# When a gate is made, where a bias row is multiplied, and where the last block's statistics and sums stand, in a conditioned two-layer block

## The chip, the cores and the metric

The kernel runs on one core of one Trainium2 chip. The core has TensorE (PE in the profile; PEld is its weight load), VectorE (DVE), ScalarE (ACT), GpSimd (POOL) and SyncE (SP), and 16 DMA engines. Each engine works through its own list of instructions in the order in which the program emits them. The metric is device time in microseconds, the median over runs.

## The reference

The input x has two batch entries of 2048 rows of 512 numbers, float32; each entry has a condition vector of 512.

```python
emb = jnp.dot(jax.nn.silu(t), ada_w) + ada_b
shift_msa, scale_msa, gate_msa, shift_mlp, scale_mlp, gate_mlp = jnp.split(emb, 6, axis=-1)
norm = _ln(x) * (1.0 + scale_msa[:, None]) + shift_msa[:, None]
h = jax.nn.gelu(jnp.dot(norm, ssm_w1) + ssm_b1, approximate=False)
x = x + gate_msa[:, None] * (jnp.dot(h, ssm_w2) + ssm_b2)
norm2 = _ln(x) * (1.0 + scale_mlp[:, None]) + shift_mlp[:, None]
hf = jax.nn.gelu(jnp.dot(norm2, ff_w1) + ff_b1, approximate=True)
x = x + gate_mlp[:, None] * (jnp.dot(hf, ff_w2) + ff_b2)
```

ssm_w1 and ssm_w2 are 512 x 512, ff_w1 is 512 x 1024, ff_w2 is 1024 x 512. Shift, scale and gate differ between the two batch entries and are the same for all rows of one. The kernel numbers the six parts of emb 0 to 5; the gates are parts 2 and 5.

## The kernel before

**Blocks and stages.** The 4096 rows are cut into eight blocks of 512; blocks 0 to 3 are batch entry 0, blocks 4 to 7 entry 1. A block i goes through four matmul stages. hA_i is norm times w1 with the first gelu. oA_i is that times w2, added to x. hC_i is the second norm times fw1 with the second gelu, in two groups of the hidden dimension. oC_i is that times fw2, added to x. The order on PE is hA_0, oA_0, hA_1, and then, for i from 0, hC_i (both groups), oA_{i+1}, oC_i, hA_{i+2}. At i = 6 there is no later hA, and oA_7 stands between the two groups of hC_6.

**Seven products.** Every stage multiplies 2 x 2 blocks with seven products P1 to P7 instead of eight (`group`, L275). Sums of quarters of the operands are formed beforehand by four additions on DVE or GpSimd (`sums_of_first`, `sums_of_second`; lines 215 to 218 and 225 to 228). The products accumulate in three PSUM banks called y, x and v: P1, P6, P7 and P4 all add into y, P2 is alone in x, P5 and P3 add into v. Partial results are read out between products, so a product that adds into a bank waits for the eviction that reads the bank's earlier state. In a hidden stage (`hidden`) DVE evicts s1 after P1 (L455) and completes it after P2 (L457), evicts u2 after P6 (L461) and completes it after P3 (L469), evicts s5 after P5 (L464) and completes it after P7 (L466); after P4 ScalarE reads the bank itself (L473). In a residual stage (`residual`) DVE adds each product's bank to x (L501). The products of most stages run in the order P1, P2, P6, P5, P7, P3, P4; the first two hidden stages and oA_0 in FIRST: P1, P2, P5, P6, P7, P3, P4.

**What sets the order.** The order is written out by hand. `hook(hooks, places, ops)` hangs other work behind a product: the operations are emitted after that product's eviction, so each engine meets them there in its own list. With more operations than places, the rest go to the last place.

**Norms.** `Norm.stats` is four statistics on DVE (L327, L328). `scales` is eight small operations on GpSimd (L336 to L354). `normal` is four instructions on ScalarE (L367). For the first blocks PE then transposes (`transpose`, L396). For later ones DVE transposes small squares (`turn`, L378), 16 DMAs on the sync queue move them (`move`, L387), and ScalarE applies scale and shift in place (`moved`, L410). `summed` forms the operand sums.

**Gates.** The gate of a part is a 512-long row for each batch entry. It is folded into the weights: w2 (and fw2) are multiplied column by column, and so is the bias row. `ada_rows` (L154) makes four partial sums for both entries with four matmuls, and adds the bias. `gates` (L198) picks and adds up one entry's rows with one matmul over 512 columns, which leaves the gate on all 128 partitions in a PSUM tile of the pool ps_t. For entry 1 it is copied into SBUF by ScalarE (L205). Both entries' gates are made at the beginning: part 2 in hA_0, part 5 in the first group of hC_0. `weight_of_second` (L253) multiplies the weights by the gate (L258) and forms the operand sums on GpSimd. When the blocks pass to entry 1, the weights are loaded afresh and folded with its gate: w2 (`refold2`) is loaded in oC_2 and folded on GpSimd during hA_4; fw2 (`refold5`) is loaded after oC_3 and folded on DVE from hC_4 on. `gate_bias` (L517) loads the bias row (`load_row`, L122) and multiplies it by the gate on GpSimd (L520); `biases` (L510) adds the product to x, four operations on GpSimd (L513). For entry 0 the row's product stands in `ssm_gate` (L643) and `gb5_0`.

Of the kernel before, what the change touches and what calls it, by code (L numbers as in the profile page):

```python
# [43 lines left out]
def kernel(  # L44
# [102 lines left out]
    load_x(1)  # L147
    b2_bc = work.tile([P, D], F32, tag="gb", name="gb2_0", bufs=2)
    load_row(b2_bc, b2)
    load_ada(3)  # L150
    load_ada(4)
    fw1_sb = load_w("fw1", fw1)

    def ada_rows(g, bias):  # L154

        pa = ps_g.tile([P, D], F32, tag="x", name=f"pada_{g}")
        for k in range(KD):
            nc.tensor.matmul(
                pa[k * G : (k + 1) * G, :],
                silu[:, k, :],  # L160
                ada[g][:, k, :],
                start=True,
                stop=True,
                tile_position=(0, k * G),
            )
        t = work.tile([P, D], F32, tag="tmp", name=f"adarows_{g}", bufs=4)
        nc.vector.tensor_tensor(t, pa, bias, ALU.add)
        return t
# [27 lines left out]
    gate = {}  # L196

    def gates(g, b, sums_g):  # L198

        pg = ps_t.tile([P, D], F32, tag="t", name=f"pgate_{g}_{b}")  # L200
        nc.tensor.matmul(pg, pick_bc[:, b, :], sums_g, start=True, stop=True)
        gate[g, b] = pg
        if b:
            gate[g, b] = work.tile([P, D], F32, tag="gate", name=f"gate_{g}_{b}", bufs=2)
            nc.scalar.activation(gate[g, b], pg, AF.Identity)  # L205
# [311 lines left out]
    def gate_bias(gt, row, name):  # L517
        t = work.tile([P, D], F32, tag="gb", name=name, bufs=2)
        load_row(t, row)
        nc.gpsimd.tensor_tensor(t, gt, t, ALU.mult)  # L520
        return t
# [118 lines left out]
    def ssm_gate():  # L640
        gates(2, 0, found["rows"])
        found["w2"] = weight_of_second(w2_sb, w2_s, gate[2, 0], (nc.vector,))
        nc.vector.tensor_tensor(b2_bc, gate[2, 0], b2_bc, ALU.mult)  # L643

    def fold2(lo, hi):
        return [lambda k=k: found["w2"][1][k]() for k in range(lo, hi)]
# [3 lines left out]
    hook(hooks, ("P2",), [lambda: found.update(rows=ada_rows(2, brows[:, 0, :]))] + n1_sums[3:])  # L650
    st = n1[1].stats()
    hook(hooks, ("P5",), [ssm_gate] + biases(0, b2_bc) + fold2(0, 2))
    hook(hooks, ("P6",), [lambda: gates(2, 1, found["rows"])] + fold2(2, 7))
    hook(hooks, ("P7",), st[:2])
    hook(hooks, ("P3",), st[2:])
    hA[0] = First(0, n1[0].ops, hooks, FIRST)
# [5 lines left out]

    hook(hooks, ("P2",), hA_sums[2:] + [lambda: modulation(3, 0)])
    hook(hooks, ("P2",), [lambda c=c: n1[1].normal(c, on_pe=True) for c in range(C)])
# [14 lines left out]
    hook(hooks, ("P6",), [lambda: found.update(rows=ada_rows(5, brows[:, 1, :]))])  # L679
# [3 lines left out]
    def ff_gate():  # L683
        for b in reversed(range(B)):
            gates(5, b, found["rows"])
        found["fw2"] = weight_of_second(fw2_sb, fw2_s, gate[5, 0], (nc.vector,))
# [21 lines left out]
    for i in range(NBLK):  # L708
# [46 lines left out]
        early = nxt and not nx2  # L755
        hooks = {}
# [37 lines left out]
        if nxt:  # L794
            run(n2[i + 1].summed(nc.vector if early else nc.gpsimd))

        refold5 = (i + 1) % PER_B == 0 and nxt
        if refold5:
            load_w("fw2", fw2, fw2_sb)
            gb[5] = gate_bias(gate[5, (i + 1) // PER_B], fb2, "gb5_1")  # L800
            fw2_ops, fold = weight_of_second(
                fw2_sb, fw2_s, gate[5, (i + 1) // PER_B], (nc.vector,)
            )
# [56 lines left out]
```

## Time and profile before

| | us |
|---|---|
| median of 3 runs | 616.57 (616.48 to 619.3) |
| the profiled execution | 616.38 |
| its span | 614.6 |
| hA_0 and oA_0 on PE | 14.5 to 47.2 |
| first product of hC_0 | from 63.8 |
| oC_2, then hA_4 | from 246.8, then from 271.0 |
| oC_3 ends, hA_5 follows | 343.5 |
| oA_7 ends, the second group of hC_6 follows | 524.8 |
| oC_6 ends, hC_7 follows | 562.0 |

A line of a group or of the timeline gives start and length (or busy time), engine, source line and operation, what it writes and reads with shapes, and in brackets the idle time before it and what ended it. The name of a tile carries its stage: py_hA is bank y of a hidden stage A. A group of a stage with four matmuls shows as x8, since one float32 matmul is two instructions here.

### The profile page before, as it was taken

The numbers are of one execution on the slowest core, as the hardware profiler recorded it, in microseconds if no ns is written. First come the engines' busy times: TensorE is split into PE (matmuls) and PEld (weight loads), VectorE is DVE, ScalarE is ACT, GpSimd is POOL, SyncE is SP. The second block draws the span as 40 slices with busy tenths as digits, with TensorE's granted clock in tenths as the row PEclk, the third lists the DMA queues.
The fourth block names the chain that finished last, engine by engine and source line by source line (L and its number), as shares of the span: only waits on it lengthen the run. The fifth ranks groups of instructions, "written<-read, shape, count | busy, mean of one in ns | idle before, by whom it ended". The sixth has DMA issues, their size and how long they took to land.

```text
span 614.6 us, 7849 instructions
## 1 busy us (share of the span) xinstructions
PE 604.0 (98%) x2899; PEld 522.5 (85%) x2899; DVE 296.3 (48%) x506; ACT 174.0 (28%) x261; POOL 354.2 (58%) x366
## 2 busy tenths in 40 slices
PE   7899999999999999999999999999999999999997
PEld 4687888888888888888888888888888888888886
DVE  5867685335553355523563367633556233714322
ACT  3234341143330531322232333115233131320110
POOL 2796489755634853549948368966555393160330
PEclk9999999999999999999999999999999999999999
DMA  8961002240113302351021820224010400021001
GB/s 326 414 254 69 1 6 64 52 154 1 28 42 78 128 2 64 91 146 61 1 68 36 251 75 18 51 63 143 1 46 24 138 1 1 6 63 68 1 2 69
DMA packets 22075, 47.74 MB, mean 78 GB/s; under 512 B 4068, under 2 KB 4624, under 8 KB 21140
## 3 DMA queue, kind: packets, MB, share of 16 engines
q1 hardware_dynamic: 21952, 47.20, 24.3%
q8 instruction: 23, 0.38, 0.3%
q14 instruction: 16, 0.13, 0.1%
q10 hardware_dynamic: 84, 0.03, 0.0%
HBM read 25.20 MB, written 8.39 MB: 55 GB/s over the span
## 4 chain that ended last, share of the span: by engine, by line
PE 92%; DMA 3%; DVE 2%; ACT 1%; SPq 1%; POOL 0%; issue 0%; ACTq 0%; DVEq 0%; POOLq 0%
PE py_oC L290 18%; PE py_hC L290 18%; PE pv_hC L290 9%; PE py_oA L290 9%; PE pv_oC L290 9%; PE py_hA L290 8%; PE pv_oA L290 5%; PE px_oC L290 4%; PE px_hC L290 4%; PE pv_hA L290 4%; PE px_oA L290 2%; DMA gb<-in_L_cond_ssm_b_dram 2%; PE px_hA L290 2%; DMA rows<-in_L_cond_ff_b_dram 1%; DVE st L327 0%; PE pt L396 0%
## 5 line engine op out<-in xcount | busy, mean ns | idle before, releaser
L410 ACT ACTIVATE nT<-nT,mod,mod 128x512 f32<-128x512 f32 x52 | 38.1, 802 | 165.1 <-DMA nT<-blocks 127.0
L513 POOL TENSOR_TENSOR x<-x,gb 128x512 f32<-128x512 f32 x64 | 79.4, 1272 | 4.0 <-issue 3.9
L215 POOL TENSOR_TENSOR hSC<-hClo 128x512 f32<-128x512 f32 x16 | 20.8, 1301 | 75.5 <-ACT hClo L450 75.5
L290 PE MATMUL py_hC<-nS,fw_s 128*128 128x256 f32 x256 | 60.7, 380 | 1.0 <-DVE s1hC L455 1.0
L367 ACT ACTIVATE nT<-x,nmr,rstd 128x512 f32<-128x512 f32 x52 | 38.7, 803 | 69.7 <-POOL nmr L354 69.7
L290 PE MATMUL py_oC<-fw_s,hSC 128*128 128x256 f32 x256 | 57.9, 379 | 0.0
L290 PEld LDWEIGHTS py_hC<-nS,fw_s 128*128 128x128 f32 x256 | 48.5, 190 | 8.3 <-DVE s1hC L455 1.8
L290 PEld LDWEIGHTS py_oC<-fw_s,hSC 128*128 128x128 f32 x256 | 48.6, 190 | 6.6
L501 DVE TENSOR_TENSOR x<-py_oC,x 128x512 f32<-128x512 f32 (+1 forms) x36 | 22.7, 631 | 64.2 <-PE py_oC L290 63.7
L225 POOL TENSOR_TENSOR nS<-nT 128x512 f32<-128x512 f32 x12 | 15.3, 1273 | 59.2 <-ACT nT L410 36.6
L327 DVE BATCH_NORM_STATS2 st<-x 128x6 f32<-128x512 f32 x64 | 43.1, 674 | 5.0 <-DMA x<-in_x_dram 4.7
L378 DVE STREAM_TRANSPOSE blocks<-nT 128x512 f32<-128x512 f32 x52 | 34.5, 691 | 6.9 <-ACT nT L367 6.9
L336 POOL TENSOR_SCALAR ve<-mv 128x4 f32<-128x4 f32 x16 | 4.0, 248 | 52.5 <-DVE mv L328 46.2
L501 DVE TENSOR_TENSOR x<-py_oA,x 128x512 f32<-128x512 f32 x32 | 22.0, 689 | 24.5 <-PE py_oA L290 23.9
L290 PE MATMUL py_hA<-nS,w_s 128*128 128x256 f32 x128 | 30.4, 381 | 1.9 <-DVE u2hA L461 1.8
L290 PE MATMUL py_oA<-w_s,hSA 128*128 128x256 f32 x128 | 30.3, 380 | 0.0
L290 PE MATMUL pv_hC<-nT,fw_s 128*128 128x256 f32 x128 | 30.3, 380 | 0.0
L290 PEld LDWEIGHTS py_hA<-nS,w_s 128*128 128x128 f32 x128 | 24.2, 190 | 7.3 <-DVE u2hA L461 3.6
L290 PE MATMUL py_hC<-nT,fw 128*128 128x256 f32 x128 | 30.2, 379 | 0.0
L290 PE MATMUL pv_hC<-nT,fw 128*128 128x256 f32 x128 | 30.2, 379 | 0.0
L290 PE MATMUL py_hC<-nS,fw 128*128 128x256 f32 x128 | 30.2, 379 | 0.0
L290 PE MATMUL px_hC<-nT,fw 128*128 128x256 f32 x128 | 30.2, 379 | 0.0
(150 smaller groups left out, 1242.4 us busy)
## 6 DMA issues: line engine op xcount, KB each, us to landing
nT<-blocks SPq DMA_DIRECT2D x208, 64.0 KB, 2.0
out_dram<-x SPq DMA_DIRECT2D x15, 512.0 KB, 7.4
x<-in_x_dram SPq DMA_DIRECT2D x7, 1024.0 KB, 6.9
ada<-in_L_cond_ada_w_dram SPq DMA_DIRECT2D x6, 1024.0 KB, 10.8
fw<-in_L_cond_ff_w_dram SPq DMA_DIRECT2D x3, 2048.0 KB, 17.1
w<-in_L_cond_ssm_w_dram SPq DMA_DIRECT2D x3, 1024.0 KB, 7.2
x<-in_x_dram SPq DMA_DIRECT2D x2, 512.0 KB, 4.6
gb<-in_L_cond_ssm_b_dram SPq DMA_DIRECT2D x2, 256.0 KB, 13.1
```

The lines of the kernel that those rows point to most:

```text
L215: lambda: eng.tensor_tensor(s[1], q["11"], q["21"], ALU.subtract),
L225: lambda: eng.tensor_tensor(s[1], q["22"], q["12"], ALU.subtract),
L290: nc.tensor.matmul(ps[b][j * apart][:, j, :], lhs(p, j, k), rhs(p, j, k), start=(fresh and j * (not apart) == 0 and k == 0), stop=(p in (" ...
L327: nc.vector.bn_stats(st, xs[self.i][:, c, :])
L336: v.tensor_scalar(ve, self.mv[:, :, 1], EPS, None, ALU.add)
L367: nc.scalar.activation(t, x_c, AF.Identity, bias=self.nmr[:, c : c + 1], scale=self.rstd[:, c : c + 1])
L378: nc.vector.transpose(self.bl[:, :, :, c, :].rearrange("p m k q -> p k m q"), self.nT[:, c, :].rearrange("p (k m q) -> p k m q", k=KD, m=C),)
L410: nc.scalar.activation(dst, src, AF.Identity, bias=shift, scale=scale)
L501: nc.vector.tensor_tensor(d, ps[BANK[p]][:, js], d, ALU.add)
L513: lambda c=c: nc.gpsimd.tensor_tensor(xs[i][:, c, :], xs[i][:, c, :], gb, ALU.add)
```

## The change

Five things. At the start the row b2 is loaded ahead of block 1's x; the row's product with the gate, and the additions on x behind it, move from behind P5 of hA_0 to behind P6; hA_0 runs P3 ahead of P7, with two statistics of block 1 behind P3 and two behind P7; the modulation of group 3's first part moves from behind P2 of oA_0 to behind P7 of hA_0. Entry 1's gates are no longer made with entry 0's: the rows are kept in SBUF (`rows_of_gates`, tile grows), and one matmul makes the gate at the switch, behind P1 of oC_2 and after oC_3; it stays in PSUM, with no copy. At the switch, the bias rows are multiplied on DVE behind P6 of oC_2 and of hA_5, fb2's row is issued ahead of fw2, the four additions on x follow there, and w2 is folded on DVE instead of GpSimd. In the last block but one, two of the four statistics of n2_7 move from oA_7's end to behind P1 of hC_6's second group. The sums of n2_7 move from after oC_6 to behind its P7 and P3.

```diff
     w2_sb = load_w("w2", w2)
-    load_x(1)
     b2_bc = work.tile([P, D], F32, tag="gb", name="gb2_0", bufs=2)
     load_row(b2_bc, b2)
+    load_x(1)
...
-    def gates(g, b, sums_g):
+    def rows_of_gates(g):
+        pa = ps_g.tile([P, D], F32, tag="x", name=f"pada_{g}")
...
+        r = work.tile([P, D], F32, tag="grows", name=f"grows_{g}", bufs=2)
+        nc.vector.tensor_tensor(r, pa, brows[:, (2, 5).index(g), :], ALU.add)
+        gate_rows[g] = r
+
+    def make_gate(g, b):
         pg = ps_t.tile([P, D], F32, tag="t", name=f"pgate_{g}_{b}")
-        nc.tensor.matmul(pg, pick_bc[:, b, :], sums_g, start=True, stop=True)
+        nc.tensor.matmul(pg, pick_bc[:, b, :], gate_rows[g], start=True, stop=True)
         gate[g, b] = pg
-        if b:
-            gate[g, b] = work.tile([P, D], F32, tag="gate", name=f"gate_{g}_{b}", bufs=2)
-            nc.scalar.activation(gate[g, b], pg, AF.Identity)
...
-    def gate_bias(gt, row, name):
-        t = work.tile([P, D], F32, tag="gb", name=name, bufs=2)
-        load_row(t, row)
-        nc.gpsimd.tensor_tensor(t, gt, t, ALU.mult)
-        return t
+    def gate_bias(g, b, row, name):
+        t = load_row(work.tile([P, D], F32, tag="gb", name=name, bufs=2), row)
+        return t, lambda: nc.vector.tensor_tensor(t, gate[g, b], t, ALU.mult)
...
     def ssm_gate():
-        gates(2, 0, found["rows"])
+        make_gate(2, 0)
         found["w2"] = weight_of_second(w2_sb, w2_s, gate[2, 0], (nc.vector,))
+
+    def gb2_0():
         nc.vector.tensor_tensor(b2_bc, gate[2, 0], b2_bc, ALU.mult)
...
-    hook(hooks, ("P2",), [lambda: found.update(rows=ada_rows(2, brows[:, 0, :]))] + n1_sums[3:])
+    hook(hooks, ("P2",), [lambda: rows_of_gates(2)] + n1_sums[3:])
     st = n1[1].stats()
-    hook(hooks, ("P5",), [ssm_gate] + biases(0, b2_bc) + fold2(0, 2))
-    hook(hooks, ("P6",), [lambda: gates(2, 1, found["rows"])] + fold2(2, 7))
-    hook(hooks, ("P7",), st[:2])
-    hook(hooks, ("P3",), st[2:])
-    hA[0] = First(0, n1[0].ops, hooks, FIRST)
+    hook(hooks, ("P5",), [ssm_gate] + fold2(0, 2))
+    hook(hooks, ("P6",), [gb2_0] + biases(0, b2_bc) + fold2(2, 7))
+    hook(hooks, ("P3", "P3", "P7"), st)
+    hook(hooks, ("P7",), [lambda: modulation(3, 0)])
+    hA[0] = First(0, n1[0].ops, hooks, ("P1", "P2", "P5", "P6", "P3", "P7", "P4"))
...
-    hook(hooks, ("P2",), hA_sums[2:] + [lambda: modulation(3, 0)])
-    hook(hooks, ("P2",), [lambda c=c: n1[1].normal(c, on_pe=True) for c in range(C)])
+    hook(hooks, ("P2",), hA_sums[2:] + [lambda c=c: n1[1].normal(c, on_pe=True) for c in range(C)])
...
     def ff_gate():
-        for b in reversed(range(B)):
-            gates(5, b, found["rows"])
+        make_gate(5, 0)
...
-            hook(hooks, ("P3", "P4"), n2[i + 1].stats())
+            st = n2[i + 1].stats()
+            hook(hooks, ("P3", "P4"), st[:2] if early else st)
+            late_stats.extend(st[2:] if early else ())
...
-            hook(hooks, ("P1",), [n2[i + 1].scales] + [lambda c=c: n2[i + 1].normal(c) for c in range(C)])
+            hook(hooks, ("P1",), late_stats + [n2[i + 1].scales])
+            hook(hooks, ("P1",), [lambda c=c: n2[i + 1].normal(c) for c in range(C)])
...
         if refold2:
+            b = (i + 2) // PER_B
+            gb[2], multiply_2 = gate_bias(2, b, b2, f"gb2_{b}")
             hook(hooks, ("P1",), [lambda: load_w("w2", w2, w2_sb)])
         if nx2:
             if refold2:
-                gb[2] = gate_bias(gate[2, (i + 2) // PER_B], b2, "gb2_1")
+                hook(hooks, ("P1",), [lambda: make_gate(2, b)])
+                hook(hooks, ("P6",), [multiply_2])
             hook(hooks, ("P1", "P2"), n1[i + 2].summed(nc.gpsimd))
-            hook(hooks, ("P2", "P6"), biases(i + 2, gb[2]))
+            hook(hooks, ("P6",) if refold2 else ("P2", "P6"), biases(i + 2, gb[2]))
...
+        if early:
+            hook(hooks, ("P7", "P7", "P3", "P3"), n2[i + 1].summed(nc.vector))
...
-        if nxt:
-            run(n2[i + 1].summed(nc.vector if early else nc.gpsimd))
+        if nx2:
+            run(n2[i + 1].summed(nc.gpsimd))
         if refold5:
+            b = (i + 1) // PER_B
+            gb[5], multiply = gate_bias(5, b, fb2, f"gb5_{b}")
             load_w("fw2", fw2, fw2_sb)
-            gb[5] = gate_bias(gate[5, (i + 1) // PER_B], fb2, "gb5_1")
+            make_gate(5, b)
...
+        if refold5:
+            hook(hooks, ("P6",), [multiply])
         if nxt:
-            hook(hooks, EARLY, biases(i + 1, gb[5]))
+            hook(hooks, ("P6",) if refold5 else EARLY, biases(i + 1, gb[5]))
         if refold2:
-            w2_ops, w2_fold = weight_of_second(w2_sb, w2_s, gate[2, (i + 2) // PER_B], (nc.gpsimd,))
+            w2_ops, w2_fold = weight_of_second(w2_sb, w2_s, gate[2, b], (nc.vector,))
```

More of the change, by code (lines that the diff above doesn't have):

```diff
@@ L152 @@
     fw1_sb = load_w("fw1", fw1)
[L154 to L167, printed above, removed]
-        return t
     mods = {}
@@ L194, in modulation @@
         mods[g0, part] = m
-    gate = {}
-    def gates(g, b, sums_g):
+    gate, gate_rows = {}, {}
+    def rows_of_gates(g):
+        pa = ps_g.tile([P, D], F32, tag="x", name=f"pada_{g}")
+        for k in range(KD):
+            nc.tensor.matmul(
+                pa[k * G : (k + 1) * G, :],
+                silu[:, k, :],
+                ada[g][:, k, :],
+                start=True,
+                stop=True,
+                tile_position=(0, k * G),
+            )
+        r = work.tile([P, D], F32, tag="grows", name=f"grows_{g}", bufs=2)
+        nc.vector.tensor_tensor(r, pa, brows[:, (2, 5).index(g), :], ALU.add)
+        gate_rows[g] = r
+    def make_gate(g, b):
         pg = ps_t.tile([P, D], F32, tag="t", name=f"pgate_{g}_{b}")
-        nc.tensor.matmul(pg, pick_bc[:, b, :], sums_g, start=True, stop=True)
+        nc.tensor.matmul(pg, pick_bc[:, b, :], gate_rows[g], start=True, stop=True)
         gate[g, b] = pg
-        if b:
-            gate[g, b] = work.tile([P, D], F32, tag="gate", name=f"gate_{g}_{b}", bufs=2)
-            nc.scalar.activation(gate[g, b], pg, AF.Identity)
     def quarters(lo, hi, a, b):
@@ L515, in biases @@
         ]
-    def gate_bias(gt, row, name):
-        t = work.tile([P, D], F32, tag="gb", name=name, bufs=2)
-        load_row(t, row)
-        nc.gpsimd.tensor_tensor(t, gt, t, ALU.mult)
-        return t
+    def gate_bias(g, b, row, name):
+        t = load_row(work.tile([P, D], F32, tag="gb", name=name, bufs=2), row)
+        return t, lambda: nc.vector.tensor_tensor(t, gate[g, b], t, ALU.mult)
     def store(i, half):
@@ L678 @@
     hook(hooks, ("P2",), biases(1, gb[2]))
-    hook(hooks, ("P6",), [lambda: found.update(rows=ada_rows(5, brows[:, 1, :]))])
+    hook(hooks, ("P6",), [lambda: rows_of_gates(5)])
     hook(hooks, ("P3", "P3", "P4", "P4"), n2[0].turned((1, 3)))
@@ L755 @@
         early = nxt and not nx2
+        late_stats = []
         hooks = {}
@@ L793 @@
             store(i, 1)
-        if nxt:
-            run(n2[i + 1].summed(nc.vector if early else nc.gpsimd))
+        if nx2:
+            run(n2[i + 1].summed(nc.gpsimd))
         refold5 = (i + 1) % PER_B == 0 and nxt
         if refold5:
+            b = (i + 1) // PER_B
+            gb[5], multiply = gate_bias(5, b, fb2, f"gb5_{b}")
             load_w("fw2", fw2, fw2_sb)
-            gb[5] = gate_bias(gate[5, (i + 1) // PER_B], fb2, "gb5_1")
-            fw2_ops, fold = weight_of_second(
-                fw2_sb, fw2_s, gate[5, (i + 1) // PER_B], (nc.vector,)
-            )
+            make_gate(5, b)
+            fw2_ops, fold = weight_of_second(fw2_sb, fw2_s, gate[5, b], (nc.vector,))
         hooks = {}
+        if refold5:
+            hook(hooks, ("P6",), [multiply])
         if nxt:
-            hook(hooks, EARLY, biases(i + 1, gb[5]))
+            hook(hooks, ("P6",) if refold5 else EARLY, biases(i + 1, gb[5]))
         if refold2:
-            w2_ops, w2_fold = weight_of_second(w2_sb, w2_s, gate[2, (i + 2) // PER_B], (nc.gpsimd,))
+            w2_ops, w2_fold = weight_of_second(w2_sb, w2_s, gate[2, b], (nc.vector,))
             hook(hooks, ALL, w2_fold)
```

## The prediction

> **What bounds the kernel now.** I read the page's first part, then the waits of TensorE, then a table of stretches, then the chain of work, and last the timeline around each place that the diff touches.
>
> ```profile
> PE 604.0 (98%) x2899; PEld 522.5 (85%) x2899; DVE 296.3 (48%) x506; ACT 174.0 (28%) x261; POOL 354.2 (58%) x366
> ```
>
> The stretches say where TensorE (PE) is not busy (columns: stretch, length, busy time and count of PE, PEld, DVE, ACT, POOL, then clock, DMA share, GB/s).
>
> ```profile
> 14.00:62.00 48.00, 45.80 (x279) 36.33 (x278) 35.20 (x61) 16.57 (x25) 36.50 (x36) 1.00 0.64 248
> 62.00:525.00 463.00, 463.00 (x2147) 406.89 (x2146) 224.01 (x373) 139.70 (x209) 292.05 (x296) 1.00 0.21 61
> 525.00:570.00 45.00, 43.97 (x202) 37.76 (x201) 18.96 (x32) 9.11 (x14) 12.46 (x16) 1.00 0.15 47
> ```
>
> From 62 to 525 us PE is busy all the time. Work taken off another engine there is worth nothing, and PE work added there is paid in full. Gaps that an edit can close exist in two places. The first is hA_0 (the chain of work; columns: start, us, what):
>
> ```profile
> 10.72 13.05 DMA gb<-in_L_cond_ssm_b_dram
> ...
> 23.86 0.23 DVE gb L643
> ...
> 24.47 1.27 DVE w L258 x2
> 25.74 0.61 DVE u2hA L461
> ...
> 26.40 1.99 PE py_hA L290 x8
> ```
>
> DVE stands still until the b2 row lands at 23.8, so the eviction u2 of P6 comes late, and P7, which adds into the bank that u2 reads, waits 1.81 us. The second place is the last block:
>
> ```profile
> 527.16 0.59 DVE st L327
> ...
> 527.87 0.68 DVE s1hC L455
> ...
> 528.60 1.99 PE py_hC L290 x8
> ...
> 534.04 1.99 PE pv_hC L290 x8
> ```
> ```profile
> 564.75 0.69 DVE nS L228
> 565.44 0.61 DVE s1hC L455
> ...
> 566.10 1.99 PE py_hC L290 x8
> ```
>
> Twice the eviction s1 is queued behind statistics or sums; PE loses 0.32 and 0.71 us. Eight matmuls that start after a wait take 1.99 us instead of 1.73: 0.26 more for a weight load that nothing covers.
>
> **The change part by part.**
>
> *The start, hA_0.* The row goes ahead of x_1's 1 MB. By the rate of that stretch (about 400 GB/s) it lands 2.6 us sooner, near 21.2. In the new order DVE does after s5 (21.35): two folds, u2 when P6 ends (23.57), then the row's product, two folds, the eviction after P3, two statistics, and only then the eviction after P7. At the pitches of the timeline (0.61 for an eviction or fold, 0.82 for a statistic with its aggregate) these start at 23.61, 24.22, 24.83, 25.44, 26.05, 26.65, 27.47 and 28.28, and the last ends at 28.97. PE now runs P3 (23.57 to 25.30) before P7 (to 27.03), then the modulation of group 3 (1.01, to 28.04). P4 adds into the bank that the last eviction reads, so it starts at 29.0 and ends at 30.99; before it ended at 31.85. That modulation needs its weights:
>
> ```profile
> ada<-in_L_cond_ada_w_dram SPq DMA_DIRECT2D x1, 1024.0 KB, 14.6
> ```
>
> Issued at 11.61, they land at 26.2, 0.8 before use; row and x_1 before them are the same bytes in either order.
>
> In oA_0 the 1.01 us of modulation is gone from between P2 and P5. It covered the second sum of hA, which P5 reads. Before, that sum ended 2.12 us after P1's end and P2 takes 1.73, so 0.4 of wait and 0.26 of uncovered weights appear. P5 ends at 36.87 against 38.24: **-1.37 us**. What is late next: GpSimd starts its four additions on x after the row's product, 25.04 against 24.69, and its eight scale operations follow in the same queue, so ScalarE's normalized x_1 is ready at 41.40 (before 41.05). PE wants it at 41.53, 0.1 later: nothing. The chain from there to the transposes at 60.44 starts with PE's own transposes and moves along with it. Bounds: -2.07 if no new wait shows (the 1.81 and 0.26), 0 if weights or normalized x come that much later.
>
> *Gates.* One gate less in front of P2 of hC_0:
>
> ```profile
> 65.38 1.88 PE L201 MATMUL pgate<-adarows,pick_bc 128*128 128x512 f32 x4
> ```
>
> P1 ends at 65.54 and P2 starts at 67.25, so two gates are 1.71 us and one 0.86: **-0.86**. The other gate that goes, after P6 of hA_0, stood in the sum above. Both come back, after P1 of oC_2 and after oC_3, where PE has no gap: **+1.72**. Two ScalarE copies (0.60 each) go, beside idle time: 0.
>
> *Folds at the switch.* Four folds of w2 move from GpSimd (1.27 each) to DVE (0.61). In hA_4 DVE has 1.03 idle before each eviction, so a fold fits behind it; w2 landed at 254.3 (issue 247.05 + 7.2), long before 271. GpSimd loses two waits for rows (11.9 and 6.4 us). PE waits for neither: 0. If that cover failed, each fold would delay PE by at most its 0.61.
>
> *The wait that is added.* DVE now multiplies gate and fb2's row after P6 of hA_5, in order, in front of the eviction s5, which frees the bank for P3. The row's way (DMA issues with us to landing; then the sync queue and DVE):
>
> ```profile
> gb<-in_L_cond_ff_b_dram SPq DMA_DIRECT2D x1, 256.0 KB, 12.6
> ```
> ```profile
> 344.73 0.45 SPq L118 DMA_DIRECT2D fw<-in_L_cond_ff_w_dram  x1
> 345.23 0.98 SPq L122 DMA_DIRECT2D gb<-in_L_cond_ff_b_dram  x1
> ```
> ```profile
> 348.74 0.69 DVE L461 TENSOR_TENSOR u2hA<-py_hA,colsT 128x512 f32<-128x512 f32 x1 [1.03 <-PE py_hA L290]
> 350.47 0.69 DVE L464 TENSOR_TENSOR s5hA<-pv_hA,colsT 128x512 f32<-128x512 f32 x1 [1.04 <-PE pv_hA L290]
> ```
>
> It lands at 357.8 behind fw2's 2.10 MB. Put ahead of them it saves 2.10 MB at the 390 GB/s of that stretch, 5.4 us, and lands near 352.4, still behind x_6's load and two stores. With the gate in front, u2 is at 349.6, s5's input is ready at 351.3, and P7 ends at 353.0. The product can start at 351.7 without harm (0.61 and s5's 0.69 behind it). At 352.4 s5 ends at 353.75, and P3 starts 0.75 late with 0.26 of weights: **+1.0**. GpSimd's additions on x_4 wait too, but start before the 359.2 of now. Bounds: 0 if the row lands by 351.7, +6.4 if it still lands with fw2 at 357.8. I take the value by queue order, since the row is now issued first. At oC_2 the same product has the row at 251.7 (GpSimd took it then) and is due after 258: 0.
>
> The Trainium skill speaks to this twice. "DMA: Bandwidth & Descriptors", in "Anatomy of one DMA", gives some 2.0 us plus bytes over 436 GB/s; that is an estimate of 2.6 us for 256 KB, a landing near 347.3 and no wait, which would make the sum +0.4 - 1.0 = -0.6. The same page, "Queues, rings and completion order", has each DMA engine take descriptors in ring order. That speaks for the queue, as does the 12.6 us of the row, nearly five times the first rule.
>
> *The last block.* Before hC_6's second group, s1 now comes ahead of two statistics: P6 starts on time (-0.32 - 0.26). But the statistics end at 528.90 instead of 527.95, 0.95 later, and behind them in one line stand eight scale operations on GpSimd (3.07 us), the normalization on ScalarE, and two transposes on DVE that are queued in front of s5, which P3 waits for. Before, P3 started exactly at s5's end (534.04 against 533.98). So it starts at 534.9: net **+0.89** at P3. The four sums go into oC_6, where DVE idles 2.7 us before each eviction; the transfers that feed them are 1.1 later, so ScalarE ends near 552, and P7's hook is at 556. Then hC_7's P6 has s1 in time: 0.71 + 0.26 = **-0.97**. Bounds together: -1.81 if the chain moves nothing, +0.9 if the sums' wait stays.
>
> **Sum:** -1.37 - 0.86 + 1.72 + 1.0 + 0.89 - 0.97 = +0.4 us. The profiled execution took 616.38 us (span 614.6, 1.8 around it), 0.2 under the median 616.57. 616.8 on that execution, 616.9 against the median.
>
> **Rivals.**
>
> *A, the row at the switch comes with its weights (slower).* The first b2 row took 13.1 us to land as well, so small rows do get held up. A landing at 357.8 stops DVE for 6.1 us with s5 and P3 behind it: +6.4 instead of +1.0, 622.3. From a landing at about 355.2 on the result is over 0.5% slower (619.65). Against it: the ring order.
>
> *B, all waits vanish (faster).* Start -2.07, gates +0.86, row 0, end -1.81: -3.0, 613.5. It needs a DVE that is never late in hA_0 and a last chain that doesn't stretch; the eight DVE operations in one row between 23.6 and 29 speak against it.
>
> *C, the start gives nothing.* GpSimd's queue or the weights of group 3 are over 1 us later than worked out: +1.4, 618.3. The 0.1 us between normalized x and PE makes some of this easy, all of it not.
>
> *D, the change does nothing anywhere*: 616.6; the order of instructions does change, so this is within the first case.
>
> **How the numbers follow.** The worked sum with its errors (615.4 to 617.7, since the start and the end may each be off by about 0.7 and the row by 0.5): 0.70. A: 0.08, of which a part lies below 619.65. B: 0.06. C: 0.16. The range 615.0 to 618.8 leaves out B, A and the tail of C. 0.5% is 3.1 us, about what a measurement of this kernel can tell from no change. Faster by more takes B and a little luck: 0.05. Slower by more takes A, or C with a late row: 0.11. Within: 0.84.
>
> **What would show it.** At the start: P7's wait for u2 gone, a wait of about 0.9 before P4 and 0.4 before P5 of oA_0, and PE at P2 of hC_0 about 2.2 us sooner. At the switch: single gates of 0.86 and, after P6 of hA_5, DVE waiting for the row near 352. At the end: hC_6's P3 waiting for s5 about 1.5 us, and hC_7's P6 for nothing. The prediction is wrong if the row lands before 351 or after 354, or if the stretch from 62 to 525 shows PE waits other than that one.

## The result, and the profile after

The changed kernel takes 618.56 us, the median of 22 runs (618.05 to 622.61), against 616.53 for the kernel before in the same runs: a ratio of 1.0032, with a 95% interval of 1.0018 to 1.0047. That is 2.03 us slower, where the sum of the prediction was +0.4. In some executions of most kernels here TensorE's granted clock is only 0.994 to 0.997 of full speed on the mean; the changed kernel's five of 22 took 0.8 to 4.1 us longer than its median. The profiled execution took 618.58 us, with a span of 616.8 at a clock of 1.00.

The first line is from the page of the changed kernel. Its TensorE works as long as before (604.0; it makes the same four gates), so the 2.2 us of span are waiting. GpSimd has 10.6 us less to do, VectorE 3.0 more.

```profile
PE 603.8 (98%) x2899; PEld 523.3 (85%) x2899; DVE 299.3 (49%) x512; ACT 173.6 (28%) x259; POOL 343.6 (56%) x360
```

The waits of TensorE in the changed kernel (us in total, times, longest):

```profile
PE pada L164 <- DMA ada<-in_L_cond_ada_w_dram: 2.0, 2, 1.4
PE pv_hC L287 <- DVE s5hC L461: 1.6, 1, 1.6
PE rowsT L584 <- DMA rows<-in_L_cond_ff_b_dram: 1.4, 1, 1.4
PE pv_oA L287 <- POOL r L335: 1.4, 1, 1.4
...
PE py_hA L287 <- DVE s5hA L463: 0.9, 1, 0.9
PE py_hA L287 <- DVE u2hA L458: 0.4, 1, 0.4
```

P7's wait of 1.81 for u2 in hA_0 is gone, and so are the two for s1, 0.32 in hC_6 and 0.71 in hC_7. In their place stand 0.9 before P4 of hA_0, 1.4 before P5 of oA_0, 0.4 before P7 of hA_1 (its u2 line), and 1.6 before P3 of hC_6. The stretch from 62 to 525 us, in which PE never stood still before, now has one gap, 0.39 of 463 us (columns as in the prediction):

```profile
62.00:525.00 463.00, 462.61 (x2142) 406.49 (x2141) 224.13 (x375) 140.44 (x209) 282.25 (x290) 1.00 0.22 61
```

PE's timeline in the changed kernel, at the places where the terms of the prediction begin and end:

```profile
15.10 1.89 PE L287 MATMUL py_hA<-nT,w 128*128 128x256 f32 x8
...
29.74 2.00 PE L287 MATMUL py_hA<-nS,w 128*128 128x256 f32 x8 [0.90 <-DVE s5hA L463]
...
36.61 1.97 PE L287 MATMUL pv_oA<-w,hA 128*128 128x256 f32 x8 [1.42 <-POOL r L335]
...
64.34 1.89 PE L287 MATMUL py_hC<-nT,fw 128*128 128x256 f32 x8
...
344.91 1.89 PE L287 MATMUL py_hA<-nT,w 128*128 128x256 f32 x8
...
354.09 2.00 PE L287 MATMUL pv_hA<-nT,w_s 128*128 128x256 f32 x8 [0.39 <-DVE s5hA L461]
...
537.24 1.99 PE L287 MATMUL pv_hC<-nT,fw_s 128*128 128x256 f32 x8 [1.58 <-DVE s5hC L461]
...
568.42 1.89 PE L287 MATMUL py_hC<-nS,fw_s 128*128 128x256 f32 x8
```

Set against the same products of the kernel before, in us from the start of each span (the starts of the timeline; the table of times before the change gives the ends of the work ahead of them, up to 0.25 us later):

| start of | before | after | later by | what the step adds |
|---|---|---|---|---|
| first product of hA_0 | 14.45 | 15.10 | 0.65 | 0.65, not predicted |
| P1 of hC_0 | 63.65 | 64.34 | 0.69 | start: +0.04 (predicted -1.37) |
| P2 of hC_0 | 67.09 | 66.92 | -0.17 | one gate less: -0.86 |
| P1 of hA_4 | 270.84 | 271.53 | 0.69 | gate in oC_2: +0.86 |
| P1 of hA_5 | 343.36 | 344.91 | 1.55 | gate after oC_3: +0.86 |
| P3 of hC_6 | 534.04 | 537.24 | 3.20 | row +0.65 (predicted 1.0), statistics +1.0 (0.89) |
| end of the span | 614.6 | 616.8 | 2.2 | sums early: -1.0 (-0.97) |

Every step after the start is within 0.4 us of its term. The start, from which the largest gain was to come, gave nothing: of its new waits one is larger than worked out, and one was not foreseen. The larger one is that before P5 of oA_0. The profile puts it down to GpSimd's r, which P5 doesn't read; P5 reads the second sum of hA, and it starts 0.15 us after that sum ends, here (36.46) as in numbers 5 and 12, whatever GpSimd operation is named. What made the sum late is in the timelines of VectorE and of GpSimd in the changed kernel:

```profile
34.17 1.10 DVE L212 TENSOR_TENSOR hSA<-hA 128x512 f32<-128x512 f32 x1
35.77 0.69 DVE L213 TENSOR_TENSOR hA<-hA 128x512 f32<-128x512 f32 x1 [0.49 <-issue]
...
33.46 1.27 POOL L224 TENSOR_TENSOR w_s<-w 128x512 f32<-128x512 f32 x1
34.81 0.55 POOL L333 TENSOR_SCALAR ve<-mv 128x4 f32<-128x4 f32 x1
```

The first sum of hA on VectorE takes 1.10 us instead of 0.68. It reads two operands from SBUF, as does GpSimd's third sum of w2, which runs beside it until 34.73. The second doesn't follow it for 0.49 us; GpSimd's small operations ve (until 35.36) and r (from 35.45) stand beside that gap. In the kernel before the same sums came when GpSimd's sum was done (33.57) and took 0.68 and 0.69, one directly after the other:

```profile
34.29 0.68 DVE L215 TENSOR_TENSOR hSA<-hA 128x512 f32<-128x512 f32 x1
35.01 0.69 DVE L216 TENSOR_TENSOR hA<-hA 128x512 f32<-128x512 f32 x1
...
32.31 1.26 POOL L227 TENSOR_TENSOR w_s<-w 128x512 f32<-128x512 f32 x1
33.66 0.23 POOL L336 TENSOR_SCALAR ve<-mv 128x4 f32<-128x4 f32 x1
33.97 1.04 POOL L338 TENSOR_TENSOR r<-ve,minus_half 128x4 f32<-128x4 f32 x1
```

### The profile page after: what moved, and what is told of

It reads as the page before. It is cut to its first block, busy times and chain, and to the rows that moved or that the text cites. A ratio compares the mean times of both kernels' runs of the same rounds, so it can differ in the third digit from the quotient of the medians.

```text
span 616.8 us, 7847 instructions
## 1 busy us (share of the span) xinstructions
PE 603.8 (98%) x2899; PEld 523.3 (85%) x2899; DVE 299.3 (49%) x512; ACT 173.6 (28%) x259; POOL 343.6 (56%) x360
## 4 chain that ended last, share of the span: by engine, by line
PE 89%; DMA 3%; DVE 3%; POOL 2%; issue 1%; ACT 1%; SPq 0%; DVEq 0%; POOLq 0%; ACTq 0%
PE py_oC L287 18%; PE py_hC L287 17%; PE pv_oC L287 9%; PE pv_hC L287 9%; PE py_oA L287 9%; PE py_hA L287 6%; PE pv_oA L287 5%; PE px_oC L287 4%; PE px_hC L287 4%; PE pv_hA L287 3%; PE px_oA L287 2%; DMA ada<-in_L_cond_ada_w_dram 2%; PE px_hA L287 1%; DMA gb<-in_L_cond_ff_b_dram 1%; PE pt L393 1%
## 5 line engine op out<-in xcount | busy, mean ns | idle before, releaser
L287 PE MATMUL pv_oC<-fw,hClo 128*128 128x256 f32 x128 | 28.9, 379 | 0.0
```

What stands on the lines that cost most here:

```text
L287: nc.tensor.matmul(ps[b][j * apart][:, j, :], lhs(p, j, k), rhs(p, j, k), start=(fresh and j * (not apart) == 0 and k == 0), stop=(p in (" ...
```

## The experiments

**Theory:** VectorE and GpSimd hold each other up when both work on operands in SBUF, and the new order of the start moved GpSimd's additions and sums onto VectorE's sums. **Rivals:** VectorE's own list is too long there (its order sets the time); the gates are what costs; the row is not sooner; or the end gives nothing. The first four kernels do parts of the change alone. The ratios are to the kernel before; a ratio is not the quotient of the two medians and can differ from it by 0.002.

**1. The row alone.** The kernel before with:

```diff
-    load_x(1)
     b2_bc = work.tile([P, D], F32, tag="gb", name="gb2_0", bufs=2)
     load_row(b2_bc, b2)
+    load_x(1)
```

> The kernel before with one edit: b2's row is loaded ahead of block 1's x. Theory: the 1.81 us wait of P7 in hA_0 and its 0.26 of uncovered weight load go, GpSimd's additions on x start about 2 us sooner as well, so nothing takes their place: 2.0 us faster than before (about 614.5), first product of hA_0 at 14.45 as before, and P5 of oA_0 without a wait of 1 us. Rival 1 (the earlier row delays the loads that the first product needs, as the first product at 15.10 instead of 14.45 in the changed kernel may mean): first product 0.65 later, gain only 1.4. Rival 2 (DVE's sums of hA and GpSimd's additions get in each other's way wherever the start is shortened): a wait of about 1 us before P5 of oA_0, gain only 1.0.

Measured: 614.57 us (11 runs) against 616.56, ratio 0.9970 (0.9956 to 0.9985). The two lines alone give the 2.0 us. PE has no wait from P5 of hA_0 to the start of hA_1, and VectorE's sums in oA_0 meet no sum of GpSimd (timelines of this kernel, whose lines are numbered as in the kernel before):

```profile
32.47 0.68 DVE L215 TENSOR_TENSOR hSA<-hA 128x512 f32<-128x512 f32 x1
33.18 0.69 DVE L216 TENSOR_TENSOR hA<-hA 128x512 f32<-128x512 f32 x1
...
30.49 1.27 POOL L227 TENSOR_TENSOR w_s<-w 128x512 f32<-128x512 f32 x1
```

**2. The sums of n2_7 early, alone.** The kernel before with:

```diff
+        if early:
+            hook(hooks, ("P7", "P7", "P3", "P3"), n2[i + 1].summed(nc.vector))
...
-        if nxt:
-            run(n2[i + 1].summed(nc.vector if early else nc.gpsimd))
+        if nx2:
+            run(n2[i + 1].summed(nc.gpsimd))
```

> The kernel before with one edit: the four sums of n2_7 stand behind P7 and P3 of oC_6 instead of after it; the statistics stay. Theory: P6 of hC_7 no longer waits, 0.97 us faster (about 615.6), the stage before unchanged. Rival (the sums in oC_6 delay its evictions): no change, 616.5.

Measured: median 617.79 us (12 runs), ratio 1.0002 (0.9984 to 1.0020). The four executions at a full clock took 614.97 to 615.54, which is the -1.0 expected; the other eight had a mean clock of 0.997, and seven of them took 617.16 to 618.78. The profiled one took 615.87, with a clock of 0.59 from 12 to 16 us; its only wait left in the last block is 0.3. The mechanism is shown; the median does not show its gain.

**3. The whole end, alone.** Number 2 with the late statistics:

```diff
-            hook(hooks, ("P3", "P4"), n2[i + 1].stats())
+            st = n2[i + 1].stats()
+            hook(hooks, ("P3", "P4"), st[:2] if early else st)
+            late_stats.extend(st[2:] if early else ())
...
-            hook(hooks, ("P1",), [n2[i + 1].scales] + [lambda c=c: n2[i + 1].normal(c) for c in range(C)])
+            hook(hooks, ("P1",), late_stats + [n2[i + 1].scales] + [lambda c=c: n2[i + 1].normal(c) for c in range(C)])
...
+        late_stats = []
```

> The kernel before with both edits of the last block: two statistics behind P1 of the second group of hC_6, and the sums behind P7 and P3 of oC_6. Theory: the later statistics cost about 1.0 at P3 of hC_6 (s5 behind the transposes) and the sums give 0.97: no change, 616.5 within 0.2, with a wait of about 1.6 us of that P3. Rival (statistics order is free, and the loss is elsewhere): 1.0 to 1.5 faster, 615.3.

Measured: 616.60 us (12 runs), ratio 1.0005 (0.9986 to 1.0023). The wait that replaces the two removed ones (waits of this kernel):

```profile
PE pv_hC L290 <- DVE s5hC L464: 1.6, 1, 1.6
```

So the two edits to the last block cancel, as predicted, to within the interval of about 1.1 us either way.

**4. The switch alone.** The changed kernel with the edits of number 3 taken back and the start put back:

```diff
+    load_x(1)
     b2_bc = work.tile([P, D], F32, tag="gb", name="gb2_0", bufs=2)
     load_row(b2_bc, b2)
-    load_x(1)
...
-    hook(hooks, ("P5",), [ssm_gate] + fold2(0, 2))
-    hook(hooks, ("P6",), [gb2_0] + biases(0, b2_bc) + fold2(2, 7))
-    hook(hooks, ("P3", "P3", "P7"), st)
-    hook(hooks, ("P7",), [lambda: modulation(3, 0)])
-    hA[0] = First(0, n1[0].ops, hooks, ("P1", "P2", "P5", "P6", "P3", "P7", "P4"))
+    hook(hooks, ("P5",), [ssm_gate, gb2_0] + biases(0, b2_bc) + fold2(0, 2))
+    hook(hooks, ("P6",), fold2(2, 7))
+    hook(hooks, ("P7",), st[:2])
+    hook(hooks, ("P3",), st[2:])
+    hA[0] = First(0, n1[0].ops, hooks, FIRST)
...
-    hook(hooks, ("P2",), hA_sums[2:] + [lambda c=c: n1[1].normal(c, on_pe=True) for c in range(C)])
+    hook(hooks, ("P2",), hA_sums[2:] + [lambda: modulation(3, 0)])
+    hook(hooks, ("P2",), [lambda c=c: n1[1].normal(c, on_pe=True) for c in range(C)])
...
```

> The changed kernel with its start and its last block put back as before: what is left is the gates of entry 1 made at the switch and kept in PSUM, the rows' products on DVE, w2 folded on DVE. Theory: 0.86 less at hC_0, 1.72 more at oC_2 and hA_5, and 0.65 for P3 of hA_5 behind the row: 1.5 us slower than before, 618.0. Rival (the matmul of a gate is worth its removal at the start, in hA_0 too): 0.65 slower, 617.2.

Measured: 621.45 us (7 runs), ratio 1.0059 (1.0033 to 1.0084); no theory expected so much. PE's timeline at hA_0, and the stretches there:

```profile
21.96 1.89 PE L287 MATMUL py_hA<-nS,w_s 128*128 128x256 f32 x8
26.01 3.65 PE L287 MATMUL py_hA<-nS,w_s 128*128 128x256 f32 x8 [2.16 <-DVE u2hA L458]
```
```profile
24.00:28.00 4.00, 1.99 (x5) 1.64 (x6) 3.15 (x6) 0.00 (x0) 3.70 (x4) 0.77 1.06 418
28.00:32.00 4.00, 4.00 (x16) 3.36 (x16) 2.24 (x6) 0.63 (x1) 3.84 (x5) 0.80 1.02 417
```

Without the second gate between P6 and P7, PE stands still for 2.16 us, and then eight matmuls take 3.65 us instead of 1.99, with a clock of 0.77 and 0.80. In this execution that is 1.7 us. The row at the switch held P3 up by 1.5 (0.39 in the changed kernel). Both together are more than the expectation had; the profiled execution took 620.30. All seven executions had a mean clock of 0.994 to 0.997, so this kernel doesn't measure the switch by itself, and why the median is another 1.2 above the profiled one is open. Number 10 measures the switch.

**5. GpSimd's sum out of the way.** The changed kernel with GpSimd's third sum of w2 in oA_0 instead of hA_0:

```diff
-    hook(hooks, ("P6",), [gb2_0] + biases(0, b2_bc) + fold2(2, 7))
+    hook(hooks, ("P6",), [gb2_0] + biases(0, b2_bc) + fold2(2, 6))
...
-    hook(hooks, ("P1",), [n1[1].scales] + fold2(7, 8) + hA_sums[:2])
+    hook(hooks, ("P1",), [n1[1].scales] + fold2(6, 8) + hA_sums[:2])
```

> The changed kernel, with GpSimd's third sum of w2 (1.27 us, 128x512) moved from behind P6 of hA_0 to oA_0. Theory: the first sum of hA on VectorE took 1.10 us because GpSimd added at the same time; with that addition away it takes about 0.69 and ends near 33.8 instead of 34.2 us, the second follows directly, and P5's wait of 1.42 us falls to 0.5 or less: about 1 us sooner at that place, 617.5 against 618.56, if the later addition delays nothing else. Rival: VectorE is late for another reason; P5's wait stays at about 1.4 us and the time at 618.5.

Measured: 620.17 us (9 runs), ratio 1.0059 (1.0041 to 1.0076): slower, against both. The timelines of VectorE, GpSimd and PE say more than the time:

```profile
33.91 0.68 DVE L212 TENSOR_TENSOR hSA<-hA 128x512 f32<-128x512 f32 x1
35.10 0.69 DVE L213 TENSOR_TENSOR hA<-hA 128x512 f32<-128x512 f32 x1 [0.51 <-issue]
...
37.10 1.77 DVE L215 TENSOR_TENSOR hSA<-hA,hSA 128x512 f32<-128x512 f32 x1
...
34.64 0.20 POOL L346 TENSOR_TENSOR e<-r 128x4 f32<-128x4 f32 x1
...
37.06 1.26 POOL L224 TENSOR_TENSOR w_s<-w 128x512 f32<-128x512 f32 x1
...
35.94 1.97 PE L287 MATMUL pv_oA<-w,hA 128*128 128x256 f32 x8 [1.01 <-POOL e L348]
38.38 1.99 PE L287 MATMUL py_oA<-w_s,hSA 128*128 128x256 f32 x8 [0.47 <-POOL w_s L224]
```

Where GpSimd's sum was taken away, VectorE's takes 0.68 instead of 1.10; where it was put, VectorE's fourth sum takes 1.77 instead of 0.69. That shows the interference. But P5's wait fell only to 1.01, since the second sum again starts half a microsecond late, with only small operations of GpSimd beside the gap (that they cause it is likely, but not shown; the profile names nothing), and P6 has a wait of 0.47. So the theory held for the mechanism and not for the gain: the collision moved along. This profiled execution took 618.91; why the median is another 1.3 above it is open.

**6. The product at the switch later.** The changed kernel with:

```diff
-            hook(hooks, ("P6",), [multiply])
+            hook(hooks, ("P4",), [multiply])
...
-            hook(hooks, ("P6",) if refold5 else EARLY, biases(i + 1, gb[5]))
+            hook(hooks, ("P4",) if refold5 else EARLY, biases(i + 1, gb[5]))
```

> The changed kernel, with the product of gate and fb2's row, and the four additions of it, behind P4 of hA_5 instead of P6: VectorE no longer stands before s5 while the row is on its way. Theory: the waits of P3 of hA_5 (0.39 and 0.26 us of uncovered weights) go, -0.65: 617.9 against 618.56. Rival: the product is late for something else, behind it in the queues (the additions to x or the sums), and the time stays at 618.5 or goes up to 619. It also gives a second look at the start of the changed kernel: first product at 15.10 us as before, or nearer to 14.45.

Measured: 617.44 us (12 runs), ratio 1.0013 (0.9995 to 1.0031), 1.1 below the changed kernel and more than the 0.65 expected (see number 9). VectorE evicts s5 at once, and P3 doesn't wait:

```profile
351.37 0.69 DVE L461 TENSOR_TENSOR s5hA<-pv_hA,colsT 128x512 f32<-128x512 f32 x1 [1.04 <-PE pv_hA L287]
...
355.43 0.68 DVE L517 TENSOR_TENSOR gb<-pgate,gb 128x512 f32<-128x512 f32 x1
```

Seven of its 12 executions lie within 617.30 to 617.48. The first product began at 14.50 here and P1 of hC_0 at 63.69, so the start's own part is -0.01 in this trace: it gives nothing even when the first loads are on time.

**7. What is left of the change when only the paying parts are taken.** The kernel before with numbers 1 and 3, and the turns of n2_7 moved out of s5's way:

```diff
-            norm_2(hooks, ("P6", "P6", "P5", "P7"), "P7")
+            norm_2(hooks, ("P5", "P5", "P7", "P7"), "P7")
```

> The kernel before, with three of the edits at once: b2's row ahead of x_1 (alone -2.0 us), the sums of hC_7's input early and in turn with VectorE's own work (alone -1.0 in the runs that no dip of the clock touched), and the late statistics with the turns of that norm moved from P6, P6, P5, P7 to P5, P5, P7, P7, so that s5 of hC_6 has no turn in front of it. Theory: the three add up, as the places are far apart: -2.0 - 1.0 - 0.6 to -0.8 = about 612.9. Rival: they don't add up at the end, since late turns make the transfers and so the sums late, and PE waits before hC_7 instead: 613.6 to 614.6, no better than the row alone.

Measured: 612.90 us (6 runs, 612.84 to 613.13) against 616.56, ratio 0.9933 (0.9913 to 0.9954), as worked out. This is the fastest kernel here, 5.7 us below the changed one. All waits of PE that are left, 3.5 us, lie ahead of hC_0:

```profile
PE pada L180 <- DMA ada<-in_L_cond_ada_w_dram: 1.9, 2, 1.4
PE idle L589 <- POOL ident masks.py:199: 1.3, 1, 1.3
PE pt L396 <- ACT blocks L367: 0.3, 1, 0.3
```

**8. The old order at the start.** The changed kernel with the lines of number 4's diff that stand below the load of the row, so that the row is still first:

```diff
...
-    hA[0] = First(0, n1[0].ops, hooks, ("P1", "P2", "P5", "P6", "P3", "P7", "P4"))
+    hA[0] = First(0, n1[0].ops, hooks, FIRST)
...
```

> The changed kernel, with the order of the start put back (P1 P2 P3-less order of before: P7 ahead of P3, product of gate and row with the additions behind P5, modulation of group 3 in oA_0), but the row still ahead of x_1. Theory: the reordered start gave nothing because of its own new waits (0.90 before P4, 1.42 before P5 of oA_0); with the old order the row alone gives its -2.0: 616.5 - 2.0 - 0.86 + 1.72 + 0.65 at the row of the switch and 0 at the end = about 616.0 to 616.9. Rival: the order of the start is free and the loss against the row alone has another cause: 618.5. A third possibility is the dip of the granted clock at 24 us that the kernel with only the switch changed showed; it would give 619 or more.

Measured: median 618.97 us (12 runs, from 617.26; four within 617.26 to 617.40), ratio 1.0031 (1.0010 to 1.0053). The profiled execution took 617.36. PE's two waits that matter:

```profile
24.55 1.99 PE L287 MATMUL py_hA<-nS,w_s 128*128 128x256 f32 x8 [0.85 <-DVE u2hA L458]
...
352.83 1.99 PE L287 MATMUL pv_hA<-nT,w_s 128*128 128x256 f32 x8 [1.67 <-DVE s5hA L461]
```

P1 of hC_0 starts at 61.80, 1.85 sooner than in the kernel before and 2.54 sooner than in the changed one, of which 0.68 is the later first product there: the reordered start does cost what the row gives. Of that gain the wait for fb2's row takes 1.3 back, 1.67 instead of 0.39. That leaves the four shortest executions 0.4 above the range of the theory; the median is nearer to the rival's 618.5, but half of the executions had a mean clock of 0.994 to 0.997, and the trace speaks for the theory. The first line tells of the gate too: P7 starts at 24.55, and in number 1, with the second gate in front of it, at 24.58. The gate that was removed from hA_0 lay in a wait.

**9. The changed kernel again,** unaltered, for a second trace.

> The changed kernel once more, unaltered, for a second trace of its start. In its first trace the first product began at 15.10 us, 0.65 later than in the kernel before, with all first loads later, although the change doesn't touch these loads; the sibling with the later product began at 14.50. If that was one execution's luck, this one begins at 14.4 to 14.6 and takes about 617.9 to 618.1; if it belongs to the program, 15.1 and 618.5 again.

Measured: 619.21 us (9 runs), ratio 1.0040 (1.0027 to 1.0052). The first product began at 14.52, so the late first loads of the first trace belong to that execution. But this one took 620.57 us, for the row at the switch:

```profile
354.74 0.69 DVE L517 TENSOR_TENSOR gb<-pgate,gb 128x512 f32<-128x512 f32 x1 [4.36 <-DMA gb<-in_L_cond_ff_b_dram]
...
356.08 1.99 PE L287 MATMUL pv_hA<-nT,w_s 128*128 128x256 f32 x8 [2.97 <-DVE s5hA L461]
```

Issued at 344.75, the row was ready at 354.74, after 10.0 us; in the first trace it took 7.4 (345.36 to 352.75), in number 8 8.7. A PE that comes there sooner has the row issued sooner by as much (in number 8 both by 2.5 us), so the wait varies with the time that the row takes. The first trace is 1.26 us longer than that of number 6: 0.60 for its later first product and 0.65 for the row. In the second, which began on time, the 3.25 over number 6 are all for the row. What the two have in the median is not shown.

**10. The gates at the switch, in the best surroundings.** Number 8 with number 6's late product and number 7's turns; against number 7 only the gates and what goes with them at the switch differ.

```diff
-            hook(hooks, ("P6",), [multiply])
+            hook(hooks, ("P4",), [multiply])
...
-            norm_2(hooks, ("P6", "P6", "P5", "P7"), "P7")
+            norm_2(hooks, ("P5", "P5", "P7", "P7"), "P7")
```

> The best of the earlier experiments (row sooner, sums early, statistics late, turns at P5, P5, P7, P7: 612.9 us) plus the main edit alone: entry 1's gates made at the switch and kept in PSUM, with fb2's product behind P4 of hA_5 so that the row holds nothing up. Theory: the gate that goes from hA_0 gives nothing, since P7 waits 0.85 for u2 there instead; the one at hC_0 gives 0.86; the two at the switch cost 1.72: 612.9 + 0.86 = 613.8, plus runs of 615 to 618 in which the granted clock dips near 24 us. Rival: the gates come out even or better, 612.9 or below.

Measured: 613.74 us (7 runs), ratio 0.9963 (0.9945 to 0.9980), 0.84 above number 7. Making entry 1's gates at the switch costs one gate, 0.86: of the two removed from the start, one was hidden.

**11. A filler.** Number 10 with:

```diff
-    hook(hooks, ("P6",), fold2(2, 7))
+    hook(hooks, ("P6",), [lambda: make_gate(2, 1)] + fold2(2, 7))
```

> The same, with two gate matmuls that nobody reads (0.86 us) put back behind P6 of hA_0, where the kernel before had its second gate. Theory of the wait: they lie in P7's wait for u2, so the quiet time is the same, 613.8. Theory of the clock: with TensorE kept busy there, the runs with a dip near 24 us (TensorE stands still for 0.85 us there without them) become fewer, and the median goes down to the quiet time. Rival: the fillers cost their 0.86, 614.7, and the dips stay as frequent.

Measured: 613.74 us (7 runs), ratio 0.9958 (0.9943 to 0.9973): the same time with two more matmuls on PE. The theory of the wait holds. That of the clock isn't decided: with the filler one of seven executions had a mean clock of 0.997, without it two of seven, too few to tell. And the dip of number 10's profiled execution isn't at 24 us at all, but ahead of the place of the filler (stretch of number 10, and below it that of number 11):

```profile
12.00:16.00 4.00, 4.00 (x44) 3.62 (x36) 1.25 (x3) 0.94 (x2) 1.46 (x2) 0.57 1.05 409
```
```profile
12.00:16.00 4.00, 4.00 (x55) 3.64 (x44) 2.46 (x5) 1.58 (x3) 1.50 (x2) 1.00 1.05 409
```

**12. VectorE relieved in hA_0.** Number 6 with:

```diff
-    hook(hooks, ("P3", "P3", "P7"), st)
+    hook(hooks, ("P7", "P7", "P4", "P4"), st)
```

> The changed kernel with the late product at the switch (617.44 us), and the statistics of x_1 moved from behind P3 and P7 of hA_0 to behind P7 and P4, so that VectorE reaches the last eviction of hA_0 1.6 us sooner. Theory (GpSimd sets the end of the start: its additions and sums share the way to memory with VectorE's sums of hA): P4's wait of 0.90 goes, but P5's wait in oA_0 grows by about as much, to 2.0 to 2.4, and the time stays at 617.2 to 617.6. Rival (VectorE's order sets it): P4's wait goes, P5's stays at 1.4, and the time falls by 0.9 to 1.2, to 616.4.

Measured: 617.05 us (12 runs, eleven of them within 616.95 to 617.16), ratio 1.0001 (0.9986 to 1.0017), 0.4 below number 6. Neither expectation holds in full (timelines of PE, then of VectorE and GpSimd):

```profile
28.19 1.99 PE L287 MATMUL py_hA<-nS,w 128*128 128x256 f32 x8
...
35.17 1.97 PE L287 MATMUL pv_oA<-w,hA 128*128 128x256 f32 x8 [1.53 <-POOL ve L333]
...
33.85 1.17 DVE L213 TENSOR_TENSOR hA<-hA 128x512 f32<-128x512 f32 x1 [0.50 <-issue]
...
48.08 1.63 DVE L222 TENSOR_TENSOR nS<-nT 128x512 f32<-128x512 f32 x1 [1.08 <-ACT nT L407]
...
46.81 2.35 POOL L215 TENSOR_TENSOR fw_s<-fw,fw_s 128x1024 f32<-128x1024 f32 x1
```

P4's wait is gone and P5's is 1.53 instead of 1.43, so P5 of oA_0 starts 0.80 sooner than in number 6, which speaks for VectorE's order. But in hA_1 VectorE's first sum of n1_1 meets GpSimd's last sum of fw1 and takes 1.63 us (1.05 in the changed kernel, 0.69 before), and at hC_0 only 0.22 of the 0.80 is left. GpSimd takes most of the gain back, one stage later than I had put it.

## Why the prediction was right or wrong

*What bounds the kernel* was right: PE's work is the same, and all of the difference is in waits, and in where the same four gates stand.

*The start* (-1.37) is the step that failed. "P7's wait gone" and "about 0.9 before P4" came as written. "0.4 of wait" before P5 of oA_0 measured 1.42. That term took VectorE's sums at 0.69 each, with nothing between them, from a trace in which GpSimd's sums of w2 were over by then. Counted from the first product, the change brings VectorE's sums 0.77 us forward and GpSimd's third sum 0.50 us back, so that the two meet (1.10, then a gap of 0.49). I did name the later GpSimd as "what is late next", but followed it only to the normalized x_1, not to what VectorE does at the same moment. One stage on, a sum of 1.05 instead of 0.69 beside GpSimd's last sum of fw1 adds 0.40 before P7 of hA_1. Together: -1.37 + 1.02 + 0.40 = +0.05, and +0.04 was measured. The measured value lies at the upper end of the bounds of -2.07 and 0, and the sign "about 2.2 us sooner" at P2 of hC_0 failed: it was 0.17, or 0.82 without the late first product. Numbers 1 and 8 show what the reordering destroyed: the row alone gives 2.0.

*Gates*: -0.86 and +1.72, as measured (number 10: +0.84 net against number 7; the gate in hA_0 was free). *Folds at the switch* at 0: right, and in a way I had not seen, told below.

*The wait that is added* (+1.0, landing near 352.4): 0.65 in the first trace (landing 352.75, with PE itself late by 1.55), 3.2 in the second, and 1.1 between the medians of the changed kernel and number 6. The size was right as a middle; the bound of 6.4 was never reached. The Trainium skill's "DMA: Bandwidth & Descriptors" ("Anatomy of one DMA"), whose fit is for single transfers that GpSimd issues, would give an estimate of 2.6 us for this size; 7.4 to 10.0 were measured for this row, which SyncE issues behind a load and two stores on the same queue. What I missed is that it varies from one execution to the next: in the second trace the row came at 354.74, past the 354 that the prediction had named as a sign of being wrong.

*The last block* (+0.89 and -0.97): +1.0 and -1.0; number 3 measures the sum as zero.

*Sum and rivals.* Two readings in the working are slightly off and change nothing: P2 of hC_0 started at 67.09 (67.25 is where the gates end), and +0.4 on the median is 617.0, not 616.9. +0.4 was predicted and +2.03 measured; with the start at 0 the same sum gives +1.8. That is the number of rival C (618.3, with a chance of 0.16), but not its mechanism. C had GpSimd's queue or the weights over 1 us later than worked out; GpSimd began its additions at 25.84, which is 25.19 without the late first product, 0.15 after the 25.04 worked out. It was VectorE that was late, beside a GpSimd that was on time. The range, which reached to 618.8, holds the time because C was priced into it, and that C's price fits is in part luck; the likeliest case did not happen. Rival A's mechanism, a row that is held up, is there in part: 10.0 us in the second trace against the 12.6 it priced.

## What to carry to other kernels

When a step moves work on GpSimd, look at what VectorE does at its new time, and price a VectorE operation with two SBUF operands there at its usual length plus up to all of the GpSimd operation beside it (here up to 1.77 instead of 0.69 us); a fold whose gate was left in PSUM was safe from this. A matmul that stands in a wait is free, and taking it away gains nothing. A product that waits for a fresh load in front of an eviction hands the spread of that load to TensorE; hang it behind the last eviction of the stage.

## What the runs showed of the hardware

**VectorE and GpSimd.** Folding fw2 shows it best: the same operation, with the gate in SBUF in the kernel before and in PSUM in the changed one. First the kernel before, then the changed kernel, each with the sum of GpSimd that runs beside the fold:

```profile
382.22 1.64 DVE L258 TENSOR_TENSOR fw<-fw,gate 128x512 f32<-128x512 f32 x1
...
382.05 1.27 POOL L216 TENSOR_TENSOR hClo<-hClo,hChi 128x512 f32<-128x512 f32 x1
```
```profile
384.43 0.68 DVE L255 TENSOR_TENSOR fw<-fw,pgate 128x512 f32<-128x512 f32 x1
...
384.43 1.27 POOL L214 TENSOR_TENSOR hSC<-hClo 128x512 f32<-128x512 f32 x1
```

With the gate in SBUF the eight folds for entry 1 took 0.68 to 1.64 us; with it in PSUM all of them took 0.68, also those that ran beside sums of GpSimd. The Trainium skill, "SBUF — State Buffer" ("SBUF: two separate sides"), gives a reason: a VectorE operation with two SBUF inputs and a GpSimd operation that reads SBUF share a pair of ports, and whichever starts first has it to its end. Most rows agree. A VectorE operation of 128x512 that is lengthened by over 0.3 us ends 0.54 to 0.56 us after the GpSimd operation beside it, however long it has taken in all: the sum of 1.10 in the changed kernel's oA_0 (35.27, against 34.73), the fold of 1.64 above (383.86, against 383.32), the sums of 1.77 in number 5 and of 1.63 in number 12. So it waits for GpSimd's end and then does its own work. GpSimd waits as well: the sum of hSA that began at 364.12 in the kernel before, while a fold ran from 363.60 to 364.72, took 1.73 us instead of 1.27. Not all rows agree: r has both operands in SBUF and runs from 33.97 to 35.01 in the kernel before, and VectorE's sum beside it took its usual 0.68. And what the gaps of half a microsecond wait for, the profile doesn't say.

**The clock.** Three of the profiled executions (numbers 2, 4 and 10) have a mean clock of 0.997. In them the clock is 0.57 to 0.80 in one or two of the stretches of 4 us between 12 and 32 us, and 0.99 or more in the others that were read. In number 10 that made 16 transposes take 3.02 us instead of 1.97 and the first product 1.55 later than in number 11. A wait of 2.16 us stood ahead of the slow matmuls at 26 us (number 4), but the kernel before waited 1.81 at the same place and had no dip; PE was busy for 1.92 of the 4 us ahead of the dip at 12 us (number 10), but number 12 had 1.82 there and no dip. What decides it was not found.
